# Keys and values of two batch elements as products of float32r halves, made in other places of the first stage

## The chip, the cores and the metric

The kernel runs on one core of a Trainium2 chip, in one launch. The metric is device time in microseconds, the median of three runs. A profile of one execution gives the times of single instructions; they are counted from the first instruction of that execution.

## The reference, cut to what matters

The input x has 4 batch elements of 512 tokens by 512 channels; ctx_2048 has the same shape. Four layers follow one another on x, each with a residual sum and a tanh gate:

```python
x = x + tanh(g_xattn[0]) * wkv_recurrence(w, u, layernorm(x), ctx_2048)   # a scan over tokens, ctx as its values
x = x + tanh(g_ffn[0])   * bitlinear_ffn(layernorm(x), w1, w2, w3)        # 512 -> 2048 -> 512, weights sign * mean
x = x + tanh(g_xattn[1]) * cross_attention(layernorm(x), ctx_2048, ...)   # 16 heads
x = x + tanh(g_ffn[1])   * ternary_linear(rmsnorm(x), gamma, W)
# within cross_attention; the query and output projections are int8 quantised, this one is not:
kv = cond @ wkv.T + bkv          # (4, 512, 512) @ (512, 1024)
k, v = split(kv, 2, axis=-1)
```

The change is in how kv is made for elements 2 and 3 (the third and fourth; counting is from 0).

## The kernel before, in words

All engines work through the four layers and four elements in one long pipeline. The first stage ("boot") holds the start, the recurrence (`wkv_layer`) of elements 0 and 1, the first feed-forward layer (`ffn_layer`) of element 0, the preparation of all weights, and the keys and values of all elements. It ends some 340 us in. Then feed-forward, attention and ternary layers of the elements run beside one another, and reread what boot left in DRAM: signs of weights (`wD`), transposed ctx (`cD`), keys (`kD`) and values (`vD`).

The order of the work is written by hand. `line(generator, parts)` gives a generator and the places of its steps; `event(place, call)` gives one call. `run` always takes the step with the lowest place, so instructions are issued in order of place. `at_unit(n)` is the place of unit n of the feed-forward layer of element 0. That layer has 16 units; a unit is one tile of 128 tokens and one block of 512 hidden channels: two products "up" (`ff_hp`), a gate, a quantisation, a transpose (`tp_ps`) and, two units later, a product "down" (`ff_acc`). Matrix instructions run strictly in that order (`in_turn` and `next_turn` tie each turn to the one before). On ScalarE, VectorE and GpSimd the tile framework orders what is ready, and these run ahead of place: the signs of the last block of w3, place 11.5, are taken at 225.0 us, before unit 10 begins at 235.5. All DMAs named here are issued from SP's queue, in order.

Keys and values (`keys_values`, lines 491 to 527): the weight wkv is transposed once into `wkvT` (f32, 16 KB per partition). ctx of an element is fetched by rows (`fetch`, tile `cn`), transposed on TensorE (`load`, `ct_ps`), copied by ScalarE to `cT` and, for elements 2 and 3, stored to `cD`. A step of keys is four f32 matmuls (128x128 weights by 512 tokens) and a `split` of the result: ScalarE writes the float32r part, VectorE the remainder, both to tile `k_half`. A step of values is four f32 matmuls and one VectorE sum (`V`). Eight steps make one element. For elements 2 and 3 they are spread over the units:

```python
for b, load, over, start in ((2, 0.7, 2.0, 3.6), (3, 9.0, 9.75, 9.8)):
    event(at_unit(load), lambda b=b: context.fetch(b))
    event(at_unit(over), lambda b=b: context.load(b))
    line(late(lambda b=b: context.keys_values(b, "m")), (at_unit(start + 0.2), at_unit(start + 6.0), 8))
```

Three things share buffers with this. `cn` of elements 2 and 3 takes one of the two buffers "wn", through which every block of weights is loaded too (`Weights.load`, line 284). A load waits until the buffer's last reader but one block is done. PSUM results of transposes, keys and values share two banks ("m"). `cT` is one buffer in the pool of boot; element 1 has its own.

Beside this, boot takes signs of the blocks of w1, w2 and w3 on ScalarE (`signs`), sums their magnitudes, turns them by bf16 transposes (`turned`, `wt_ps`), and from unit 11 on loads wq, wp and wf, quantises them on VectorE (`rounded`, `ternary`: lines 218 to 220 are `quantise`), and turns them into `wqT`, `wpT`, `wfT` (`ints_turned`). `output_scales` fills `swp_b` and `bp_b`. These five constants are first written after unit 12.

Of the kernel before, what the change touches and what calls it, by code (L numbers as in the profile page):

```python
# [10 lines left out]
F32 = mybir.dt.float32  # L11
# [10 lines left out]
P = 128  # L22
# [8 lines left out]
def kernel(  # L31
# [69 lines left out]
    wqT = cp.tile([P, NC, D], BF16, name="wqT")  # L101
    wpT = cp.tile([P, NC, D], BF16, name="wpT")
    wfT = cp.tile([P, NC, D], BF16, name="wfT")
# [7 lines left out]
    bp_b = cp.tile([P, D], F32, name="bp_b")  # L111
    gamma_b = cp.tile([P, D], F32, name="gamma_b")
    sq = cp.tile([P, NC], F32, name="sq")
    swp_b = cp.tile([P, D], F32, name="swp_b")
# [159 lines left out]
    class Weights:  # L274
# [134 lines left out]
        def ints_turned(self, key):  # L409
            dst = {"q": wqT, "p": wpT, "f": wfT}[key]  # L410
            yield from self.transposed(self.ints.pop(key), lambda c: dst[:, c, :], 0)

        def output_scales(self):

            pb = bank("pb_ps")
            for j in range(NC):
                transpose(
                    pb[:, j * P : (j + 1) * P],
                    self.sp[:, j : j + 1].to_broadcast([P, P]),
                    ident,  # L420
                )
            nc.vector.tensor_scalar(swp_b, pb, gates[:, 1:2], None, ALU.mult)
# [4 lines left out]
    class Context:  # L427


        def __init__(self, pool):  # L430
# [4 lines left out]
            self.wkvT = pool.tile([P, NC, 2 * D], F32, name="wkvT")  # L435
# [49 lines left out]
        def weights_turned(self, i):  # L485
            wn = self.raw[i]
            for j in range(NC):
                at = i * D + j * P
                self.transposed(self.wkvT[:, :, at : at + P], wn[:, j, :])

        def keys_values(self, b, tag):
# [3 lines left out]
            for g in range(NC):  # L495
                kp = psum_tile("k_ps", tag)
                for c in range(NC):
                    matmul(
                        kp,
                        lhsT=self.wkvT[:, c, g * P : (g + 1) * P],  # L500
# [11 lines left out]
            for t in range(NT):  # L512
                vp = psum_tile("v_ps", "m" if b else tag)
                for c in range(NC):
# [3 lines left out]
                        rhs=self.wkvT[:, c, D : 2 * D],  # L518
# [301 lines left out]
    def attention_layer(b, xb, pool, tiles=range(NT)):  # L820
# [18 lines left out]
        def prepared(t, r):  # L839
# [13 lines left out]
            nc.gpsimd.tensor_tensor(xb[:, t, :], xb[:, t, :], bp_b, ALU.add)  # L853
# [12 lines left out]
        def project(g):  # L866
            qp = bank("q_ps")[:, 0:n]
            for c in range(NC):
                matmul(
                    qp,  # L870
                    lhsT=wqT[:, c, g * P : (g + 1) * P],
# [124 lines left out]
        def project_out(t):  # L996
# [10 lines left out]
            for c in range(NC):  # L1007
                matmul(
                    pp, lhsT=oqT[:, c, :], rhs=wpT[:, c, :], start=(c == 0), stop=(c == NC - 1)
# [5 lines left out]
            nc.vector.scalar_tensor_tensor(y, pp, s[:, 0:1], swp_b, ALU.mult, ALU.mult)  # L1015
# [88 lines left out]
    def ternary(b, xb, pool, t, r, scale=None):  # L1104
# [38 lines left out]
        for c in range(NC):  # L1143
            matmul(fp, lhsT=xT[:, c, :], rhs=wfT[:, c, :], start=(c == 0), stop=(c == NC - 1))
# [55 lines left out]
    with (  # L1200
# [81 lines left out]
        for b, load, over, start in ((2, 0.7, 2.0, 3.6), (3, 9.0, 9.75, 9.8)):  # L1282
            event(at_unit(load), lambda b=b: context.fetch(b))
            event(at_unit(over), lambda b=b: context.load(b))
            line(
                late(lambda b=b: context.keys_values(b, "m")),
                (at_unit(start + 0.2), at_unit(start + 6.0), 8),
# [107 lines left out]
```

## Time and profile before

| | us |
|---|---|
| three runs | 1115.97, 1114.70, 1111.44 |
| median | 1114.7 |
| the profiled execution, whole | 1115.4 |
| its span, first to last instruction | 1113.6 |
| TensorE busy in the span | 946.8 (85%) |
| VectorE busy | 851.9 (76%) |
| ScalarE busy | 704.8 (63%) |
| GpSimd busy | 315.3 (28%) |
| mean granted TensorE clock | 0.953 of full |

How to read it: the engines run beside one another, so busy times do not add up to the span. The time of a matmul in the trace goes from its start to its last result, and the next one starts before that; the time between two starts is what one costs in a row. A clock under 1.00 is what the chip's throttle granted to TensorE. In lists by time, the bracket behind an instruction says how long its engine sat idle and what ended that.

### The profile page before, as it was taken

How to read it: one execution, taken by the hardware profiler on the slowest of the kernel's cores; microseconds unless marked ns; L12 is line 12 of the kernel's file. 1: busy time of each engine (PE TensorE's matmuls, PEld its weight loads, DVE VectorE, ACT ScalarE, POOL GpSimd, SP SyncE). 2: the span in 40 equal slices, each digit the busy share in tenths (PEclk: the TensorE clock that was granted, in tenths of full speed). 3: DMA queues.
4: the chain of work that ended last, by engine and by line, in shares of the span. 5: the costliest groups of instructions: out<-in, count | busy, mean ns of one | idle time of the engine just before them, and what ended most of it. 6: DMA issues, size and time to landing. Idle time of an engine off the chain costs nothing.

```text
span 1113.6 us, 17974 instructions
## 1 busy us (share of the span) xinstructions
PE 946.8 (85%) x6380; PEld 683.5 (61%) x6380; DVE 851.9 (76%) x1642; ACT 704.8 (63%) x1454; POOL 315.3 (28%) x311
## 2 busy tenths in 40 slices
PE   4879998978878978889998777899998989878885
PEld 3345565555546756667776466677776767656652
DVE  4986447779776799988759988877687766679977
ACT  6756655453224676667777667577775677877864
POOL 3822104432105143542214536412113321100000
PEclk8879999998888999999999999999998999989997
DMA  8189854554435655644746544466564653253411
GB/s 283 50 275 319 305 199 147 179 170 152 151 104 170 226 188 161 195 152 158 246 153 209 178 152 152 145 213 199 170 197 152 225 193 109 71 158 106 114 49 39
DMA packets 85673, 189.68 MB, mean 170 GB/s; under 512 B 12240, under 2 KB 36816, under 8 KB 74576
## 3 DMA queue, kind: packets, MB, share of 16 engines
q1 hardware_dynamic: 85584, 188.53, 51.5%
q8 instruction: 51, 0.84, 0.3%
q14 instruction: 38, 0.31, 0.1%
HBM read 148.65 MB, written 39.85 MB: 169 GB/s over the span
## 4 chain that ended last, share of the span: by engine, by line
PE 44%; DVE 25%; ACT 12%; issue 8%; POOL 6%; DMA 3%; SPq 1%; POOLq 0%; ACTq 0%; DVEq 0%
PE ff_hp L162 13%; PE ff_acc L162 6%; PE pt_ps L165 5%; PE o_ps L162 4%; PE s_ps L162 3%; PE v_ps L162 3%; DVE wk_q L620 3%; ACT at_P L929 3%; DVE at_nm L927 3%; ACT at_PT L949 2%; PE k_ps L162 2%; PE tp_ps L165 2%; DVE wk_p L614 2%; DVE qg_i L660 1%; PE qr_ps L165 1%
## 5 line engine op out<-in xcount | busy, mean ns | idle before, releaser
L162 PE MATMUL ff_hp<-wT,xp 128*128 128x512 f32 x1024 | 273.7, 411 | 3.7 <-ACT at_P L929 2.1
L162 PEld LDWEIGHTS ff_hp<-wT,xp 128*128 128x128 f32 x1024 | 197.4, 196 | 52.4 <-ACT at_P L929 3.8
L929 ACT ACTIVATE at_P<-s_ps,at_nm 128x512 f32<-128x512 f32 x256 | 174.6, 689 | 74.6 <-DVE at_nm L927 70.9
L927 DVE TENSOR_REDUCE at_nm<-s_ps 128x1 f32<-128x512 f32 x256 | 165.6, 676 | 37.8 <-PE s_ps L162 37.2
L665 POOL TENSOR_TENSOR ff_z<-qg_b,qg_s 128x512 f32<-128x512 bf16 x64 | 71.4, 1116 | 333.0 <-ACT qg_b L664 286.6
L165 PE MATMUL pt_ps<-ident,at_P 128*128 128x128 f32 x1024 | 141.1, 278 | 17.5 <-ACT at_os L969 6.6
L949 ACT COPY at_PT<-pt_ps 128x512 f32<-128x512 f32 x224 | 124.5, 595 | 39.7 <-PE pt_ps L165 38.5
L165 PEld LDWEIGHTS pt_ps<-ident,at_P 128*128 128x128 f32 x1024 | 113.2, 140 | 45.6 <-issue 9.3
L162 PE MATMUL ff_acc<-wT,hr 128*128 128x512 f32 x512 | 136.9, 408 | 4.9 <-ACT hr L676 3.0
L162 PE MATMUL s_ps<-at_kR,at_qR 128*128 128x512 f32 x256 | 98.8, 455 | 22.2 <-ACT at_P L929 14.6
L162 PEld LDWEIGHTS ff_acc<-wT,hr 128*128 128x128 f32 x512 | 92.6, 190 | 25.5 <-ACT hr L676 4.1
L725 ACT ACTIVATE ff_z<-ff_hp,coef 128x512 f32<-128x512 f32 x64 | 43.9, 687 | 65.8 <-PE ff_hp L162 63.2
L162 PE MATMUL o_ps<-at_PT,at_V 128*32 128x128 f32 x2048 | 72.2, 279 | 1.3 <-DVE hr L677 0.7
L664 ACT CAST qg_b<-qg_i 128x512 bf16<-128x512 int8 x80 | 49.3, 617 | 35.3 <-DVE qg_i L660 27.4
L162 PEld LDWEIGHTS s_ps<-at_kR,at_qR 128*128 128x128 f32 x256 | 46.2, 196 | 38.7 <-ACT at_P L929 23.6
L730 DVE SCALAR_TENSOR_TENSOR ff_z<-ff_hp,coef,ff_z 128x512 f32<-128x512 f32 x64 | 47.5, 743 | 28.2 <-PE ff_hp L162 28.2
L162 PE MATMUL v_ps<-wkvT,cT 128*128 128x512 f32 x128 | 63.8, 646 | 5.6 <-DVE wT L301 2.3
L162 PEld LDWEIGHTS o_ps<-at_PT,at_V 128*32 128x32 f32 x2048 | 53.8, 111 | 23.9 <-issue 12.2
L726 DVE SCALAR_TENSOR_TENSOR ff_z<-ff_z,ff_hp 128x512 f32<-128x512 f32 x64 | 43.4, 678 | 29.7 <-ACT ff_z L725 29.1
L165 PE MATMUL tp_ps<-ident,ff_z 128*128 128x128 f32 x256 | 41.3, 286 | 26.3 <-ACT at_PT L949 11.3
L162 PE MATMUL k_ps<-cT,wkvT 128*128 128x512 f32 x128 | 60.1, 620 | 3.1 <-ACT cT L444 1.4
L676 ACT CAST hr<-tp_ps 128x512 fp32r<-128x512 f32 x64 | 37.6, 587 | 35.8 <-PE tp_ps L165 35.5
(180 smaller groups left out, 1683.1 us busy)
## 6 DMA issues: line engine op xcount, KB each, us to landing
wT<-wD SPq DMA_DIRECT2D x72, 1024.0 KB, 5.3
wn<-in_L_ffn_w_dram SPq DMA_DIRECT2D x18, 1024.0 KB, 6.3
at_kR<-kD SPq DMA_DIRECT2D x128, 128.0 KB, 3.2
at_qR<-qD SPq DMA_DIRECT2D x256, 64.0 KB, 2.3
wD<-wT SPq DMA_DIRECT2D x12, 1024.0 KB, 4.5
kD<-k_half SPq DMA_DIRECT2D x16, 512.0 KB, 3.0
qD<-at_half SPq DMA_DIRECT2D x32, 256.0 KB, 2.1
cn<-in_ctx_dram SPq DMA_DIRECT2D x8, 512.0 KB, 6.3
```

Of the source, the lines that this page charges most:

```text
L162: return in_turn(nc.tensor.matmul(*args, **kwargs))
L165: return in_turn(nc.tensor.transpose(*args))
L620: nc.vector.reciprocal(half, half)
L664: nc.scalar.copy(qb, qi)
L665: nc.gpsimd.tensor_tensor(grouped(src), grouped(qb), s.unsqueeze(2).to_broadcast([P, NG, GS]), ALU.mult)
L676: nc.scalar.copy(part[:, 0, :], pt)
L725: nc.scalar.activation(z, hp, AF.Tanh, scale=coef[:, 0:1])
L726: nc.vector.scalar_tensor_tensor(z, z, 1.0, hp, ALU.add, ALU.mult)
L730: nc.vector.scalar_tensor_tensor(z, hp, coef[:, 1:2], z, ALU.mult, ALU.mult)
L927: nc.vector.tensor_reduce(nm, sp, AX.X, ALU.max, negate=True)
L929: nc.scalar.activation(lanes[k, i, t], sp, AF.Exp, bias=nm, accum_out=sums[k][:, t, i : i + 1],)
L949: made[k] = nc.scalar.copy(dst, blocks(pt))
```

## The change

For elements 2 and 3 keys and values are no longer made by f32 matmuls. wkv and ctx are each written as a float32r part and a remainder, and three float32r products (high by high, high by low, low by high) are summed in PSUM.

- `split_weights(i)`, i = 0 for the key half and 1 for the value half of wkv: 4 ScalarE copies to a tile `w_hi` and 4 VectorE subtractions to `w_lo` (128x512 each); then a DMA of 1 MB copies `w_hi` over the f32 weights. The remainders lie in the memory of `wqT`, `wpT`, `wfT`, `bp_b` and `swp_b`, which are now allocated when first written.
- `fetch_half(b, h)` reads 256 tokens of the transposed ctx back from `cD` (512 KB); `split_half` splits them by two ScalarE copies and a VectorE subtraction over 1024 columns.
- `half_keys_values(b, h)` has four steps: two with the keys of two groups of 128 channels each (24 matmuls over 256 columns, two splits), two with the values of a tile of tokens (12 matmuls over 512 columns, one sum). Key results are stored by DMAs half as large.
- `w_hi`, the pair of ctx halves and the `cT` of elements 2 and 3 all use the one buffer "cT".
- ctx of element 3 is fetched at place 3.0 in place of 9.0, and transposed at 3.5 in place of 9.75. The weights are split at 3.8 and 4.7, and the four half-elements stand at 6.2, 7.9, 9.6 and 11.3, one unit each.

The core of the diff:

```diff
-    wqT = cp.tile([P, NC, D], BF16, name="wqT")
-    wpT = cp.tile([P, NC, D], BF16, name="wpT")
-    wfT = cp.tile([P, NC, D], BF16, name="wfT")
+    turned_ints = {}
...
         def ints_turned(self, key):
-            dst = {"q": wqT, "p": wpT, "f": wfT}[key]
+            name = f"w{key}T"
+            dst = cp.tile([P, NC, D], BF16, name=name, tag=name)
+            turned_ints[key] = dst
             yield from self.transposed(self.ints.pop(key), lambda c: dst[:, c, :], 0)
 
         def output_scales(self):
...
+            swp_b = cp.tile([P, D], F32, name="swp_b", tag="swp_b")
+            bp_b = cp.tile([P, D], F32, name="bp_b", tag="bp_b")
+            turned_ints["scale"], turned_ints["bias"] = swp_b, bp_b
...
-            self.wkvT = pool.tile([P, NC, 2 * D], F32, name="wkvT")
+            self.W = [
+                pool.tile([P, NC, D], F32, name="wkvT", tag=f"wkvT{i}") for i in range(2)
+            ]
+            self.low = {}
...
         def weights_turned(self, i):
             wn = self.raw[i]
             for j in range(NC):
-                at = i * D + j * P
-                self.transposed(self.wkvT[:, :, at : at + P], wn[:, j, :])
+                self.transposed(self.W[i][:, :, j * P : (j + 1) * P], wn[:, j, :])
+
+        def split_weights(self, i):
+
+            W = self.W[i]
+            high = self.pool.tile([P, NC, D], F32R, name="w_hi", tag="cT")
+            for c in range(NC):
+                tag = (("wqT", "wpT"), ("wfT", ("bp_b", "swp_b")))[i][c // 2]
+                if isinstance(tag, tuple):
+                    lo = cp.tile([P, D], F32R, name="w_lo", tag=tag[c % 2])
+                elif c % 2 == 0:
+                    both = cp.tile([P, 2, D], F32R, name="w_lo", tag=tag)
+                    lo = both[:, 0, :]
+                else:
+                    lo = both[:, 1, :]
+                nc.scalar.copy(high[:, c, :], W[:, c, :])
+                nc.vector.tensor_tensor(
+                    lo, W[:, c, :], high[:, c, :].bitcast(F32), ALU.subtract
+                )
+                self.low[i, c] = lo
+                if c % 2:
+                    yield
+            self.W[i] = self.pool.tile([P, NC, D], F32R, name="w_high", tag=f"wkvT{i}")
+            nc.sync.dma_start(out=self.W[i].bitcast(F32), in_=high.bitcast(F32))
+
+        def fetch_half(self, b, h):
+
+            self.pair = self.pool.tile([P, 2, NC, 2 * P], F32, name="c_pair", tag="cT")
+            cut = slice(2 * P * h, 2 * P * (h + 1))
+            nc.sync.dma_start(out=self.pair[:, 0], in_=cD[b][:, :, cut])
+
+        def split_half(self):
+
+            hi, lo = self.pair[:, 0], self.pair[:, 1]
+            nc.scalar.copy(lo.bitcast(F32R), hi)
+            nc.vector.tensor_tensor(lo.bitcast(F32R), hi, lo, ALU.subtract)
+            nc.scalar.copy(hi.bitcast(F32R), hi)
+
+        def half_keys_values(self, b, h):
+
+            hi, lo = self.pair[:, 0], self.pair[:, 1]
+            cut = slice(2 * P * h, 2 * P * (h + 1))
+            store = lambda: None
+
+            def products(out, c, w, ctx):
+                i, w = w.start // D, slice(w.start % D, w.start % D + w.stop - w.start)
+                high = self.W[i][:, c, w], ctx(hi)
+                low = self.low[i, c][:, w], ctx(lo)
+                for n, (x, y) in enumerate(((0, 0), (0, 1), (1, 0))):
+                    weight, context = (high, low)[x][0], (high, low)[y][1]
+                    pair = (context, weight) if i else (weight, context)
+                    matmul(
+                        out,
+                        lhsT=pair[0].bitcast(F32R),
+                        rhs=pair[1].bitcast(F32R),
+                        start=(c == 0 and n == 0),
+                        stop=(c == NC - 1 and n == 2),
+                    )
+
+            for g2 in range(0, NC, 2):
+                kp = psum_tile("k_ps", "m")
+                half = self.pool.tile([P, 2, 2, 2 * P], F32R, name="k_half", tag="k_half", bufs=2)
+                for g in (g2, g2 + 1):
+                    out = kp[:, (g - g2) * 2 * P : (g - g2 + 1) * 2 * P]
+                    for c in range(NC):
+                        products(out, c, slice(g * P, (g + 1) * P), lambda a: a[:, c, :])
+                    split(half[:, g - g2], out, self.bkc[:, g : g + 1])
+                store()
+
+                def store(g2=g2, half=half):
+                    for g in (g2, g2 + 1):
+                        nc.sync.dma_start(
+                            out=kD[b][g][:, :, cut].rearrange("i p t -> p i t"),
+                            in_=half[:, g - g2].bitcast(F32),
+                        )
+
+                yield
+            for j in range(2):
+                t = 2 * h + j
+                vp = psum_tile("v_ps", "m")
+                for c in range(NC):
+                    products(
+                        vp,
+                        c,
+                        slice(D, 2 * D),
+                        lambda a: a[:, c, j * P : (j + 1) * P],
+                    )
+                V = self.pool.tile([P, D], F32, name="V", tag="k_half", bufs=2)
+                nc.vector.tensor_tensor(V, vp, self.bv_b, ALU.add)
+                store()
+                store = lambda t=t, V=V: nc.sync.dma_start(out=vD[b][:, t, :], in_=V)
+                yield
+            store()
 
         def keys_values(self, b, tag):
 
...
-                        lhsT=self.wkvT[:, c, g * P : (g + 1) * P],
+                        lhsT=self.W[0][:, c, g * P : (g + 1) * P],
...
-                        rhs=self.wkvT[:, c, D : 2 * D],
+                        rhs=self.W[1][:, c, :],
...
             event(at_unit(sign), lambda m=m, f=f: made.signs(m, f, m == 2))
             line(made.turned(m, f), (at_unit(end - 0.8), at_unit(end + 0.1), 4))
         event(at_unit(12.0), made.down_scale)
-        for b, load, over, start in ((2, 0.7, 2.0, 3.6), (3, 9.0, 9.75, 9.8)):
+        for b, load, over in ((2, 0.7, 2.0), (3, 3.0, 3.5)):
             event(at_unit(load), lambda b=b: context.fetch(b))
             event(at_unit(over), lambda b=b: context.load(b))
+        for i, start in enumerate((3.8, 4.7)):
             line(
-                late(lambda b=b: context.keys_values(b, "m")),
-                (at_unit(start + 0.2), at_unit(start + 6.0), 8),
+                late(lambda i=i: context.split_weights(i)),
+                (at_unit(start), at_unit(start + 0.4), 3),
+            )
+        for b, h, start, end in (
+            (2, 0, 6.2, 7.2),
+            (2, 1, 7.9, 8.9),
+            (3, 0, 9.6, 10.6),
+            (3, 1, 11.3, 12.3),
+        ):
+            event(at_unit(start - 0.65), lambda b=b, h=h: context.fetch_half(b, h))
+            event(at_unit(start - 0.35), context.split_half)
+            line(
+                late(lambda b=b, h=h: context.half_keys_values(b, h)),
+                (at_unit(start), at_unit(end), 4),
             )
         for key, w, load in (("q", wq, 11.0), ("p", wp, 12.1), ("f", wf, 13.3)):
             event(at_unit(load), lambda key=key, w=w: made.load(key, w))
```

More of the change, by code (lines that the diff above doesn't have):

```diff
@@ L110 @@
     bqc = cp.tile([P, NC], F32, name="bqc")
-    bp_b = cp.tile([P, D], F32, name="bp_b")
     gamma_b = cp.tile([P, D], F32, name="gamma_b")
     sq = cp.tile([P, NC], F32, name="sq")
-    swp_b = cp.tile([P, D], F32, name="swp_b")
     coef = cp.tile([P, 4], F32, name="coef")
@@ L851, in prepared @@
             nc.scalar.copy(sxb[:, t * P : (t + 1) * P], sp)
-            nc.gpsimd.tensor_tensor(xb[:, t, :], xb[:, t, :], bp_b, ALU.add)
+            nc.gpsimd.tensor_tensor(xb[:, t, :], xb[:, t, :], turned_ints["bias"], ALU.add)
             yield True
@@ L870, in project @@
                     qp,
-                    lhsT=wqT[:, c, g * P : (g + 1) * P],
+                    lhsT=turned_ints["q"][:, c, g * P : (g + 1) * P],
                     rhs=xqT[:, c, lo : lo + n],
@@ L1008, in project_out @@
                 matmul(
-                    pp, lhsT=oqT[:, c, :], rhs=wpT[:, c, :], start=(c == 0), stop=(c == NC - 1)
+                    pp, lhsT=oqT[:, c, :], rhs=turned_ints["p"][:, c, :], start=(c == 0), stop=(c == NC - 1)
                 )
@@ L1014, in project_out @@
                 y = row("at_y")
-            nc.vector.scalar_tensor_tensor(y, pp, s[:, 0:1], swp_b, ALU.mult, ALU.mult)
+            nc.vector.scalar_tensor_tensor(y, pp, s[:, 0:1], turned_ints["scale"], ALU.mult, ALU.mult)
             (nc.vector if b > NB - 3 else nc.gpsimd).tensor_tensor(
@@ L1143, in ternary @@
         for c in range(NC):
-            matmul(fp, lhsT=xT[:, c, :], rhs=wfT[:, c, :], start=(c == 0), stop=(c == NC - 1))
+            matmul(fp, lhsT=xT[:, c, :], rhs=turned_ints["f"][:, c, :], start=(c == 0), stop=(c == NC - 1))
         xt = xb[:, t, :]
```

## The prediction

> **What bounds the kernel now.** First the page's 40 slices, to find the changed stage.
>
> ```profile
> PE   4879998978878978889998777899998989878885
> DVE  4986447779776799988759988877687766679977
> ACT  6756655453224676667777667577775677877864
> PEclk8879999998888999999999999999998999989997
> ```
>
> A slice is 27.8 us. All that changes lies in slices 3 to 12, the stage in which the first feed-forward layer runs over 16 units while weights are prepared and keys and values of elements 2 and 3 are made. TensorE is busiest of the engines to slice 9; in slices 8 and 9 (222 to 278 us) VectorE reaches 9 too, and in slices 9 to 12 the granted clock sinks. So I cut the stage at first matmuls of feed-forward units (unit 3 at 137.8 us, 6 at 178.5, 10 at 235.5, 12 at 265.0, 15 at 318.4, the layer after at 344.2) and read busy time in these five stretches, A to E:
>
> ```profile
> 137.80:178.50 40.70, 36.71 (x177) 24.11 (x173) 22.07 (x35) 25.24 (x39) 7.70 (x8) 1.00 0.53 199
> 178.50:235.50 57.00, 49.39 (x227) 32.02 (x225) 39.55 (x53) 29.91 (x47) 20.02 (x21) 1.00 0.44 150
> 235.50:265.00 29.50, 23.39 (x100) 15.62 (x98) 27.55 (x42) 9.67 (x19) 11.02 (x10) 0.94 0.53 187
> 265.00:318.40 53.40, 42.59 (x177) 27.15 (x176) 45.61 (x96) 12.97 (x21) 13.05 (x12) 0.86 0.33 116
> 318.40:344.20 25.80, 20.76 (x78) 13.59 (x76) 15.79 (x42) 6.84 (x12) 8.03 (x9) 0.83 0.55 168
> ```
>
> After length come TensorE, weight loads, VectorE, ScalarE, GpSimd, then clock. A and B are TensorE's (90% and 87%); C is VectorE's (93%); D is shared, VectorE 85%, with TensorE at a clock of 0.86; E is a tail of short chains. A microsecond of TensorE is therefore worth most in A and B, one of VectorE in C and D.
>
> Next, TensorE in order of time, for what a product costs when others follow at once (a duration in the trace overlaps the next one, so I use starts):
>
> ```profile
> 132.16 3.59 PE L162 MATMUL v_ps<-wkvT,cT 128*128 128x512 f32 x8
> 135.59 0.60 PE L165 MATMUL tp_ps<-ident,ff_z 128*128 128x128 f32 x4
> ...
> 193.38 3.98 PE L162 MATMUL ff_hp<-wT,xp 128*128 128x512 f32 x16
> 197.19 0.60 PE L165 MATMUL wy_ps<-ident,wk_e 128*128 128x128 f32 x4
> 197.63 3.60 PE L162 MATMUL v_ps<-wkvT,cT 128*128 128x512 f32 x8
> ...
> 283.21 6.77 PE L162 MATMUL v_ps<-wkvT,cT 128*128 128x512 f32 x8 [0.68 <-ACT wqT L299]
> ...
> 321.91 4.41 PE L162 MATMUL v_ps<-wkvT,cT 128*128 128x512 f32 x8
> 326.16 0.39 PE L165 MATMUL wt_ps<-identb,wi 128*128 128x128 bf16 x4
> 326.36 2.11 PE L162 MATMUL ff_hp<-wT,xp 128*128 128x512 f32 x8
> ```
>
> A step of keys or values (four f32 products, two records each) takes 135.59 - 132.16 = 3.43 us. A float32r product over 512 columns takes (197.19 - 193.38)/16 = 0.238 us. A 128x128 transpose, each with a weight load of its own, takes (197.63 - 197.19)/4 = 0.11 us.
>
> Last, the loads, for what holds the quantisation that fills VectorE in C and D:
>
> ```profile
> 195.54 1.73 SPq L458 DMA_DIRECT2D cn<-in_ctx_dram  x2
> 215.80 0.38 SPq L286 DMA_DIRECT2D wn<-in_L_ffn_w_dram  x1
> 231.11 0.38 SPq L286 DMA_DIRECT2D wn<-in_L_xattn_wq_dram  x1
> ```
> ```profile
> 237.46 2.29 DVE L214 TENSOR_REDUCE w_am<-wn 128x4 f32<-128x2048 f32 x1 [0.63 <-DMA wn<-in_L_xattn_wq_dram]
> ```
>
> wq's load leaves at 231.11, when the fourth element's ctx (cn), loaded at 195.5 into one of two "wn" buffers, has been transposed (230.43 + 0.65). VectorE then waits for wq's data.
>
> **The change, part by part.** *Products.* Out: 16 steps of 3.43 = 54.9 us. In: for keys 192 products over 256 columns, each with its own weight load; no row shows this form. It lies between the transpose's 0.11 us (a load, 128 columns) and the 0.238 us of 512 columns; I take half of the latter, 0.119, since the load of 0.11 fits behind it: 24 per step, 2.86 us. For values 12 per step over 512 columns, 2.86 us. Sum 45.8 us, 9.1 less, if it holds. The upper end is 24 x 0.238 = 5.7 us per key step, 23 us more in all. The Trainium skill (TensorE: Matmul & The Clock Gate, Part 3) says that a weight load overlaps a running matmul only when the row groups differ, which would put load and stream end to end. The trace disagrees: ff_hp loads full 128 rows (187 ns recorded) and still starts a product every 238 ns. By that rule a key step would be near the upper end.
>
> *Places.* Before, one step falls every 0.725 unit from place 3.8 to 15.8: A holds 4 key steps, B 4 value and 1 key, C 2 key, D 1 key and 3 value, E 1 value. After, four bursts of four steps stand from place 6.2 to 12.05: A none, B 10 steps, C 5, D 1, E none.
>
> *Splitting.* ScalarE gets 8 copies of 128x512 (0.59 us, as hr L676) and 8 of 128x1024 (1.05, as wk_e L594): 13 us. VectorE gets 8 subtractions of 0.69 (as V L523) and 4 of 1024 columns at 1.22 (two of 0.69 less a fixed part, by the line from 512 to the 2.29 of 2048): 10.4 us. Halving the key splits doubles their fixed parts: 16 more instructions of some 0.15 us each (the near-empty ones of 128x4 take that) on both engines, 2.4 us or less. So VectorE +13, ScalarE +15 over A to C. In A ScalarE is 62% busy, VectorE 54%: covered by TensorE there. Where that cover goes, as in C, each costs itself.
>
> *ctx sooner.* 16 transposes (4 x 0.44 = 1.8 us of TensorE, 2.4 of ScalarE copies) move from B to A. cn leaves the ring of loads, so wq follows the matrix whose signs end at 215.8, not cn: its load can leave 15 us earlier, and wp and wf after it. wq's quantisation is 2.28 + 4 x (0.48 + 0.41 + 0.41) = 7.5 us of VectorE that can slide from C and D into B, where VectorE has 17 us free. The new DMAs (two of 1 MB within SBUF, four ctx halves back from cD) add some 4 MB to a stage whose DMA share is 0.33 to 0.55; their price is latency, below. Key stores double in number, half in size: 8 more issues of 0.35 us on SP, which is idle between.
>
> *Waits.* All of it uses one buffer, "cT": cD's store of the fourth ctx (7.1 us to landing), split, copy back (1 MB; 4.2 as wD's store to 7.1), split, copy, fetch of a half (3.0 as kD's store to 5.3 as cn's), its split (2 x 1.05 + 1.22). Sum 7.1 + 4 + 5.5 + 4 + 5.5 + 4 + 3.3 = 33 us, from the ctx transposes at place 3.5 to the first keys at 6.2: 2.7 units, at A's 13.6 us each 37 us. It just fits; it fits no longer if A shrinks by more than 4 us. Behind a late split stand, on TensorE, all matmuls in turn; on SP, behind a fetch waiting for the previous half's last product, the weight loads and stores.
>
> *By stretch.*
> A: four steps out, of which the chain of waits carries two (3.70 + 3.45); transposes in. TensorE busy falls to 36.7 - 13.7 + 1.8 = 24.8, ScalarE rises to 25.2 - 2.1 + 2.4 + 4.7 + 2.1 = 32.3. Between -7 and +5; I take -2.5, held up by the chain just named.
> B: TensorE 49.4 - 17.2 - 1.8 + 28.6 = 59.0. With all 7.6 us of present idle kept 66.6, with none 59; VectorE's slack fills some. I take 62.5, +5.5.
> C: TensorE 23.4 - 6.9 + 14.3 = 30.8, VectorE 27.6 + 4 less what slid to B. I take 32, +2.5 (ends +1 and +4).
> D: TensorE 42.6 - 17.8 (the rows' busy time, slow clock included) + 2.9 = 27.7; VectorE 45.6 - 2.8 + 0.7 - up to 7.5 = 36 to 43.5, and the idle waits of VectorE for v_ps (1.9 + 0.6 + 0.2) go. I take 44.4, -9 (ends -14 and -4): what is late next is VectorE.
> E: v_ps at 321.91 stands between the two feed-forward products of the last unit; the second moves up by 326.36 - 321.91 less the transposes, 4.2 us. I take -4 (ends -5 and -2).
> Sum -2.5 + 5.5 + 2.5 - 9 - 4 = -7.5. The profiled execution took 1115.4 (span 1113.6, 1.8 around it), 0.7 above the median of 1114.7, so 1114.7 - 7.5 = 1107. Ends: -24 and +13 together, neither likely.
>
> D's clock speaks against it. The row is v_ps at 283.21: 6.77 us for what takes 3.6, after idle of 3.54 us, at a mean clock of 0.86. The skill's same page (Part 1) says a window of about 3.4 us without work halves the clock. By the row kept as it is, D gives -9; by the rule, with filler gone, each further such window at half clock loses 1.7 us, and two bring D to -5.6 and the sum to -4.
>
> **The rivals.** *Given back, no change (0.27).* TensorE's total falls by 9 us but VectorE's rises by 13, of which 6.7 falls in A, and with five more steps B to D are nearly VectorE's: 39.6 + 27.6 + 45.6 + 10 = 123 of 139.9 us. If nothing slides, D gives -5, B +8, C +3, A -2.5, E -3: 1115. For it: C's 93%; against: the free 17 us in B, which wq reaches earlier.
> *The single buffer, slower (0.28).* TensorE's order is fixed, so the burst at 6.2 waits when the chain of 33 us ends after TensorE reaches it, that is once A is under 36.7 us; then each refill (fetch 3 to 5.3, split 3.3, queueing) must fit 0.95 unit, 13 us. With 4 us in A in place of the gain (+6.5) and 3 at each of three refills (+9): 1107 + 15.5 = 1122.
> *Products over 256 columns dearer (0.03).* At 5.7 us a key step the change doesn't do what it says: 1107 + 23 = 1130.
>
> **How the numbers follow.** Forecast, faster: 0.42. About 0.5%, 5.6 us, is what a measurement of this kernel can tell from no change, so "same" is 1109 to 1120. Faster 0.42, same 0.27, slower 0.28 + 0.03 = 0.31. The range takes D's and A's better ends (1107 - 10) and the buffer rival with 2 us more: 1097 to 1124. The forecast's own range is 1097 to 1109.
>
> **What would show it.** Right: key products start every 0.12 us, value products every 0.24; wq's load leaves near 215 us; no v_ps after unit 13; D and E together are 10 us or more shorter, B is 4 to 8 longer. Wrong: TensorE idle before the first k_ps of a burst, released by ScalarE's or VectorE's c_pair (the buffer); D as long as before with VectorE over 90% (given back); key products at 0.2 us or more.

## The result: slower by 2.3%, and where the time went

The changed kernel took 1139.4 us (median of four runs, 1137.5 to 1142.0) beside 1113.6 us for the kernel before (four runs, 1111.4 to 1116.0): a ratio of 1.023 with an interval of 1.020 to 1.026. The profiled execution took 1142.0, its span is 1140.2. The forecast was 1107, the range ended at 1124. In what follows "over before" is the ratio less one, times 1114 us; here that is +26 us.

The page's slices, which are now 28.5 us long:

```profile
PE   4879974796885988888999788799999989878885
DVE  5976465568688688998677998877677775669977
ACT  6756674434422566676786756677766676887863
PEclk8879995997988899999999999999999999999998
```

In slices 6 to 9 (counted from 0; 171 to 285 us), where TensorE was at 7 to 9 before, it shows 4, 7, 9, 6, and the clock falls to 5 in slice 6. The same five stretches A to E as before, cut at the same feed-forward units (length, then busy time of TensorE, weight loads, VectorE, ScalarE, GpSimd, then clock, DMA share and GB/s):

```profile
138.40:172.70 34.30, 26.68 (x161) 21.04 (x159) 20.48 (x36) 23.82 (x38) 3.58 (x5) 0.93 0.72 258
172.70:277.90 105.20, 73.32 (x364) 61.04 (x362) 67.08 (x90) 45.22 (x71) 32.00 (x31) 0.76 0.40 141
277.90:313.00 35.10, 30.73 (x168) 24.64 (x167) 21.43 (x42) 13.14 (x21) 2.09 (x2) 0.96 0.45 152
313.00:351.40 38.40, 28.49 (x155) 22.15 (x156) 35.48 (x74) 10.33 (x17) 13.57 (x11) 0.88 0.33 115
351.40:373.00 21.60, 15.27 (x71) 10.78 (x68) 16.81 (x46) 6.59 (x12) 9.35 (x10) 0.90 0.56 184
```

Against before A is 6.4 us shorter, B 48.2 longer, C 5.6 longer, D 15.0 and E 4.2 shorter: +28.2 in all. What lies around the stretches gives 1.6 back, which makes the 26.6 us by which the span grew. Nearly all that is lost is lost in B. There TensorE is idle for 31.9 us (7.6 before), and its own 73.3 us of work run at a clock of 0.76.

What TensorE waited for in B, the list's first lines (total us, times, longest):

```profile
PE k_ps L158 <- ACT c_pair L528: 20.6, 3, 12.6
PE k_ps L158 <- DVE k_half L252: 9.9, 7, 2.7
```

These two waits make 30.5 of the 31.9 us. The first is the buffer "cT": TensorE stands before a half until ScalarE's last split of it. The second stands inside the half, six of its seven times between the two groups of a key step. In TensorE's order of time (start, us, and the wait in the bracket):

```profile
189.54 0.80 PE L158 MATMUL k_ps<-c_pair,w_high 128*128 128x256 f32 x2 [12.64 <-ACT c_pair L528]
...
190.35 0.63 PE L158 MATMUL k_ps<-c_pair,w_high 128*128 128x256 f32 x2
190.78 0.41 PE L158 MATMUL k_ps<-c_pair,w_lo 128*128 128x256 f32 x1
190.99 0.63 PE L158 MATMUL k_ps<-c_pair,w_high 128*128 128x256 f32 x2
...
193.56 0.80 PE L158 MATMUL k_ps<-c_pair,w_high 128*128 128x256 f32 x2 [1.08 <-DVE k_half L252]
...
196.28 3.06 PE L158 MATMUL ff_hp<-wT,xp 128*128 128x512 f32 x8
...
199.40 0.48 PE L158 MATMUL k_ps<-c_pair,w_high 128*128 128x256 f32 x2
...
199.83 0.39 PE L158 MATMUL k_ps<-c_pair,w_high 128*128 128x256 f32 x2
200.06 0.28 PE L158 MATMUL k_ps<-c_pair,w_lo 128*128 128x256 f32 x1
200.18 0.40 PE L158 MATMUL k_ps<-c_pair,w_high 128*128 128x256 f32 x2
...
202.13 0.50 PE L158 MATMUL k_ps<-c_pair,w_high 128*128 128x256 f32 x2 [1.08 <-DVE k_half L252]
```

Between the groups of the last pair, ScalarE in order of time:

```profile
201.09 0.47 ACT L251 ACTIVATE k_half<-k_ps,bkc 128x256 fp32r<-128x256 f32 x1 [4.09 <-PE k_ps L158]
```

and VectorE half a microsecond later:

```profile
201.59 0.48 DVE L252 SCALAR_TENSOR_TENSOR k_half<-k_ps,bkc,k_half 128x256 fp32r<-128x256 f32 x1
```

The two groups of a key step share one bank tile of PSUM ("kp"). The second group's first product writes that tile, so it waits until the first group's split has read it: ScalarE at 201.09, then VectorE at 201.59, then TensorE at 202.13. At full clock three products take 200.18 - 199.83 = 0.35 us, 0.117 each; after the long wait 190.99 - 190.35 = 0.64, 0.213 each. Of the 16 key groups seven run at the slow pace from end to end, and one in part.

How a split comes late: ScalarE's order of time in front of the first half,

```profile
181.95 1.03 ACT L526 CAST c_pair<-c_pair 128x1024 fp32r<-128x1024 f32 x1
188.45 1.04 ACT L528 CAST c_pair<-c_pair 128x1024 fp32r<-128x1024 f32 x1 [5.46 <-DVE c_pair L527]
```

and VectorE's:

```profile
180.51 3.33 DVE L715 RECIPROCAL wk_q<-wk_q 128x256 f32<-128x256 f32 x2
185.47 1.23 DVE L674 TENSOR_TENSOR_SCAN wk_o<-wc,wk_k 128x512 f32<-128x512 f32 x1 [1.63 <-POOL wk_p L683]
186.61 0.67 DVE L720 TENSOR_TENSOR wk_e<-wk_e,wk_q 128x512 f32<-128x512 f32 x1
187.19 1.22 DVE L527 TENSOR_TENSOR c_pair<-c_pair 128x1024 fp32r<-128x1024 f32 x1
```

ScalarE had its first cast done at 183.0. VectorE came to the subtraction at 187.2, behind the recurrence of element 1, in which it even sat idle for 1.63 us. Last, SP's queue in order of time:

```profile
171.12 0.48 SPq L515 DMA_DIRECT2D w_high<-w_hi  x1
176.42 0.60 SPq L521 DMA_DIRECT2D c_pair<-cD  x1
...
214.80 0.55 SPq L521 DMA_DIRECT2D c_pair<-cD  x1
...
246.12 0.38 SPq L282 DMA_DIRECT2D wn<-in_L_xattn_wq_dram  x1
```

The first fetch leaves 5.3 us after the copy back of the high weights, which had to free the buffer. The second leaves at 214.80, 1.2 us after the first half's last product has ended, right behind the store of its values. wq's load leaves at 246.1, not near 215: the signs of the block before it end at 246.1 (ScalarE, 244.18 + 1.91).

### The profile page after: what moved, and what is told of

Read it like the earlier page. It is cut to its first block, busy times and chain, and to the rows that moved or that the text cites. A ratio compares the mean times of both kernels' runs of the same rounds, so it can differ in the third digit from the quotient of the medians.

```text
span 1140.2 us, 18387 instructions
## 1 busy us (share of the span) xinstructions
PE 948.3 (83%) x6540; PEld 710.8 (62%) x6540; DVE 862.1 (76%) x1662; ACT 718.6 (63%) x1478; POOL 315.9 (28%) x311
## 4 chain that ended last, share of the span: by engine, by line
PE 47%; DVE 22%; ACT 13%; issue 7%; POOL 6%; DMA 5%; SPq 1%; POOLq 0%; ACTq 0%; DVEq 0%
PE ff_hp L158 13%; PE ff_acc L158 5%; PE pt_ps L161 5%; PE k_ps L158 4%; PE o_ps L158 4%; PE s_ps L158 4%; PE v_ps L158 3%; ACT at_P L1024 3%; ACT at_PT L1044 2%; DVE wk_q L715 2%; DVE at_nm L1022 2%; PE tp_ps L161 2%; PE qr_ps L161 2%; DVE wk_p L709 2%; DVE qg_i L755 1%
## 5 line engine op out<-in xcount | busy, mean ns | idle before, releaser
L158 PEld LDWEIGHTS ff_hp<-wT,xp 128*128 128x128 f32 x1024 | 199.7, 199 | 49.2 <-ACT at_P L1024 3.8
L1022 DVE TENSOR_REDUCE at_nm<-s_ps 128x1 f32<-128x512 f32 x256 | 165.6, 676 | 37.5 <-PE s_ps L158 36.8
L825 DVE SCALAR_TENSOR_TENSOR ff_z<-ff_hp,coef,ff_z 128x512 f32<-128x512 f32 x64 | 47.5, 742 | 29.5 <-PE ff_hp L158 29.4
L771 ACT CAST hr<-tp_ps 128x512 fp32r<-128x512 f32 x64 | 37.5, 586 | 41.0 <-PE tp_ps L161 40.7
L161 PE MATMUL tp_ps<-ident,ff_z 128*128 128x128 f32 x256 | 41.3, 286 | 24.2 <-ACT at_PT L1044 11.0
L158 PE MATMUL k_ps<-c_pair,w_high 128*128 128x256 f32 x128 | 33.3, 360 | 33.4 <-ACT c_pair L528 21.3
L715 DVE RECIPROCAL wk_q<-wk_q 128x256 f32<-128x256 f32 x32 | 54.4, 1719 | 2.6 <-POOL wk_p L703 1.4
```

The costliest lines, as they stand in the source:

```text
L158: return in_turn(nc.tensor.matmul(*args, **kwargs))
L161: return in_turn(nc.tensor.transpose(*args))
L715: nc.vector.reciprocal(half, half)
L771: nc.scalar.copy(part[:, 0, :], pt)
L825: nc.vector.scalar_tensor_tensor(z, hp, coef[:, 1:2], z, ALU.mult, ALU.mult)
L1022: nc.vector.tensor_reduce(nm, sp, AX.X, ALU.max, negate=True)
```

## The experiments

Length of each stretch in us, cut at the same units, and the time over before with the ends of its interval (the ratio of each kernel is to runs of before on the same chip):

| kernel | A | B | C | D | E | median | over before |
|---|---|---|---|---|---|---|---|
| before | 40.7 | 57.0 | 29.5 | 53.4 | 25.8 | 1113.6 | |
| after | 34.3 | 105.2 | 35.1 | 38.4 | 21.6 | 1139.4 | +26 (22 to 29) |
| e1, splits last | 35.0 | 87.8 | 41.3 | 37.5 | 21.3 | 1129.0 | +14 (7 to 20) |
| e2, two buffers | 36.7 | 85.7 | 34.3 | 38.6 | 21.8 | 1125.1 | +10 (7 to 13) |
| e3, both | 35.7 | 73.8 | 38.4 | 38.3 | 21.6 | 1116.9 | +1 (-2 to 5) |
| e4, ctx sooner alone | 47.0 | 51.5 | 29.4 | 54.2 | 24.9 | 1116.6 | +2 (0 to 5) |
| e5, f32 in bursts | 29.4 | 74.8 | 41.7 | 38.2 | 21.3 | 1114.4 | 0 (-2 to 2) |
| e6, halves spread | 47.8 | 66.9 | 35.4 | 38.6 | 21.6 | 1117.3 | +3 (1 to 5) |
| e7, one product | 35.0 | 59.3 | 26.6 | 47.2 | 22.2 | 1099.6 | -15 (-18 to -12) |
| e8, no remainders | 32.9 | 78.8 | 35.2 | 37.5 | 22.5 | 1114.2 | 0 (-2 to 3) |
| e9, GpSimd subtracts | 36.8 | 81.5 | 37.6 | 37.5 | 21.3 | 1123.0 | +9 (6 to 12) |
| e10, f32 in e3's form | 33.0 | 81.3 | 42.4 | 40.3 | 21.3 | 1125.2 | +11 (9 to 14) |
| e11, high parts only | 33.1 | 64.0 | 28.5 | 46.0 | 22.3 | 1102.7 | -12 (-14 to -9) |
| e12, whole elements | 31.8 | 58.0 | 29.7 | 47.5 | 22.1 | 1097.6 | -18 (-21 to -15) |

**The three theories of the loss.** R: the refill of the one buffer. B: the bubble between the two groups of a key step. V: VectorE is full anyway, and time taken from either wait comes back elsewhere. Later expectations name their theories by letters too: P for the places of the products, S for the splitting, L and C for what cheaper products are worth; each says what it means where it first stands.

e1, both groups multiplied before either is split:

```diff
+                outs = [kp[:, i * 2 * P : (i + 1) * 2 * P] for i in range(2)]
                 for g in (g2, g2 + 1):
-                    out = kp[:, (g - g2) * 2 * P : (g - g2 + 1) * 2 * P]
                     for c in range(NC):
-                        products(out, c, slice(g * P, (g + 1) * P), lambda a: a[:, c, :])
-                    split(half[:, g - g2], out, self.bkc[:, g : g + 1])
+                        products(outs[g - g2], c, slice(g * P, (g + 1) * P), lambda a: a[:, c, :])
+                for g in (g2, g2 + 1):
+                    split(half[:, g - g2], outs[g - g2], self.bkc[:, g : g + 1])
```

> The changed kernel, with the two key groups of a step multiplied one after the other and both split behind them; all else as in the changed kernel (1139.4 us). Theory R (refill: the changed kernel loses its time where TensorE waits for the one buffer of ctx halves, 21.3 us of waits for c_pair, and in the slow clock behind each of them): the 12.1 us of waits inside key steps go, the rest stays, so 1127 to 1137. Theory B (bubble: the wait of the second group for the split of the first, 1.1 to 2.7 us in each of 8 key steps, is what breaks the bursts and keeps the clock down): 1139 less 12 us of waits less most of the 14 us of slow clock, 1113 to 1122. Theory V (the added work of VectorE and ScalarE, 13 and 15 us, is the loss): 1139 within 3.

Measured 1129.0. From e1's list of TensorE's waits over A to E, the line for the splits of ctx:

```profile
PE k_ps L158 <- ACT c_pair L528: 16.7, 4, 12.7
```

The refills still wait for 16.7 us (21.3 in after), 12.7 of it at the first. Waits for splits of keys fall from 12.1 to 7.7 us: none stands inside a step any more, and two are left behind a step. So most of the 10 us gained (12 by the two ratios) are the bubble's, with the slow clock behind it. The time lies in R's range; V falls, and B alone (1113 to 1122) falls too.

e2, the first half of each element in memory of its own (that of x of element 2, which is loaded later), so that it is fetched and split ahead:

```diff
-            self.pair = self.pool.tile([P, 2, NC, 2 * P], F32, name="c_pair", tag="cT")
+            pool, tag = (self.pool, "cT") if h else (st, "x2")
+            pair = pool.tile([P, 2, NC, 2 * P], F32, name="c_pair", tag=tag, bufs=1)
...
-            event(at_unit(start - 0.65), lambda b=b, h=h: context.fetch_half(b, h))
-            event(at_unit(start - 0.35), context.split_half)
+            event(at_unit(start - 2.0), lambda b=b, h=h: context.fetch_half(b, h))
+            event(at_unit(start - 0.9), lambda b=b, h=h: context.split_half(b, h))
```

> The changed kernel, with the halves h = 0 of ctx in a second buffer (the memory that later takes x of the third element), each half fetched 2.0 units and split 0.9 units ahead of its products; the products, their places and the work of VectorE and ScalarE are the same. Theory R: the waits for c_pair (21.3 us) go, and the clock behind them (up to 14 us) returns: 1104 to 1120. Theory B: 1134 or more, since the bubbles stay. Theory V: 1139 within 3.

Measured 1125.1, 14 us less than after. The head of e2's list of the same waits:

```profile
PE k_ps L158 <- DVE k_half L252: 19.2, 10, 4.1
```

No wait for c_pair is left, and the bubble has grown from 12.1 (over A to E) to 19.2 us: in the longest, 4.07 us, VectorE runs a scan and a reciprocal of the recurrence (1.97 and 1.72 us) before it comes to the split. R's range (1104 to 1120) was too hopeful, B's (1134 or more) is out.

e3 has both edits.

> Both edits together: a second buffer for ctx halves, fetched earlier, and splits behind both key groups. Theories R and B add: 1098 to 1112, below the kernel before (1113.6). Theory V: 1136 or more.

Measured 1116.9: 22.5 us less than after, where the two gains alone add up to 24.7. So the two waits are two causes, about 14 and 10 us (16 and 12 by the ratios, 24.5 together), each with the slow clock that follows it. Waits for splits of keys are not gone: 8.5 us of them stand in e3 before the second key step of a half or before its values. But 1116.9 is no gain over before, and above the expected 1098 to 1112. Next question: why is nothing left of the 9 us that the products save?

**Is it the places?** e4 is before with ctx of element 3 fetched and transposed at 3.0 and 3.5, stored, and read back at 9.75; the f32 steps stay where they were.

```diff
-        for b, load, over, start in ((2, 0.7, 2.0, 3.6), (3, 9.0, 9.75, 9.8)):
+        for b, load, over, start in ((2, 0.7, 2.0, 3.6), (3, 3.0, 3.5, 9.8)):
...
+            if b == 3:
+                event(at_unit(9.75), lambda b=b: context.again(b))
```

> The kernel before (1113.6 us), with f32 products in their old places, but ctx of the fourth element fetched at place 3.0 and transposed at 3.5 into memory of x of the third element, stored, and read back (1 MB) into cT at 9.75: the part 'ctx loaded sooner' alone. If the 15 us that stretch D (units 12 to 14) lost in the changed kernel come from wq's earlier load, D loses 5 us or more here too: 1104 to 1110. If they come from the products moved out of D, D stays as it was: 1111 to 1117.

Measured 1116.6. wq's load left at 220.5 in place of 231.1, and D and E together are 79.1 us, as before (79.2). An earlier wq is worth nothing here; D's gain is from the products that moved out.

e5 adds two bursts of f32 steps to that, 6.2 to 8.9 and 9.6 to 12.3, with no splitting at all; ctx of element 3 is read back at 9.0.

```diff
-                (at_unit(start + 0.2), at_unit(start + 6.0), 8),
+                (at_unit(start), at_unit(start + 2.7), 8),
```

> The kernel before with f32 products, ctx of the fourth element sooner (as in e4), and the 16 steps in two bursts of 8 at places 6.2 to 8.9 and 9.6 to 12.3, in place of 3.8 to 15.8: the change of places alone, with no splits of weights or ctx and no refill of halves. Theory P (places: what e3 still loses in units 6 to 11 is crowding of the products, whatever their form): 16 steps of 3.43 us in the bursts against 2.86 in e3 (1116.9 us) make 1122 to 1130. Rival S (splitting: the 13 and 15 us of added work on VectorE and ScalarE eat what the products save): 1112 to 1119, no slower than e3.

Measured 1114.4, in the range of S, with no sign of P. The five stretches of e5, with the same columns as above:

```profile
138.70:168.00 29.30, 24.86 (x159) 19.49 (x157) 16.08 (x28) 19.14 (x29) 3.48 (x4) 1.00 0.81 293
168.00:242.90 74.90, 65.84 (x253) 38.74 (x250) 53.18 (x74) 37.90 (x60) 24.18 (x25) 0.98 0.44 161
242.90:284.50 41.60, 36.35 (x132) 20.53 (x130) 28.23 (x47) 11.44 (x18) 9.55 (x10) 1.00 0.45 158
284.50:322.70 38.20, 25.58 (x145) 19.92 (x144) 34.24 (x72) 9.52 (x16) 13.44 (x10) 0.85 0.28 97
322.70:344.00 21.30, 15.21 (x71) 11.02 (x69) 16.80 (x46) 6.59 (x11) 9.83 (x10) 0.90 0.65 197
```

A, D and E lose 31 us and B and C gain 30. The burst costs in B and C what it frees in A, D and E, to a microsecond. Places are worth nothing either way, and e6 says the same of e3, with its halves at 5.2 to 7.0, 7.0 to 8.8, 8.9 to 10.6 and 10.7 to 12.4:

```diff
-            (2, 0, 6.2, 7.2),
-            (2, 1, 7.9, 8.9),
-            (3, 0, 9.6, 10.6),
-            (3, 1, 11.3, 12.3),
+            (2, 0, 5.2, 7.0),
+            (2, 1, 7.0, 8.8),
+            (3, 0, 8.9, 10.6),
+            (3, 1, 10.7, 12.4),
```

> e3 (two buffers, splits behind both groups) with the four halves spread without gaps over places 5.2 to 12.4, one step every 0.45 unit in place of bursts of four at every 0.25. Theory P: TensorE's idle in stretch A is filled and units 6 to 9 shorten; 4 to 10 us less than e3, 1107 to 1113, below the kernel before (1114.2). Rival S: as e3, 1114 to 1119.

Measured 1117.3, again where S had it.

**Is it the products?** e7 keeps one product of the three, high by high, and all of e3's splitting.

```diff
-                for n, (x, y) in enumerate(((0, 0), (0, 1), (1, 0))):
+                for n, (x, y) in enumerate(((0, 0),)):
```

> e3 with only the high by high product of the three; the two products with a remainder are left out, all splits stay. TensorE has 30 us less to do in units 6 to 12. Theory P: these units are TensorE's, so 18 to 30 us less than e3: 1087 to 1099. Rival S: they are VectorE's (93 us busy of 112 in units 6 to 11 of e3), so less than 12 us: 1105 to 1116.

Measured 1099.6, 17 us less than e3 for 30 us less of products. That lies between the two ranges: TensorE's time counts, by about half of what is taken out.

e10 goes the other way: e3's form, but one f32 product of the high parts in place of the three, about 9 us more.

```diff
-                for n, (x, y) in enumerate(((0, 0), (0, 1), (1, 0))):
+                for n, (x, y) in enumerate(((0, 0),)):
...
-                        lhsT=pair[0].bitcast(F32R),
-                        rhs=pair[1].bitcast(F32R),
+                        lhsT=pair[0].bitcast(F32),
+                        rhs=pair[1].bitcast(F32),
```

> The kernel e3_both with its splitting, buffers, places and steps unchanged, but each sum of three float32r products replaced by one f32 product of the high parts (the remainders are made and not used). By before's rows an f32 step takes 3.43 us where three float32r products take 2.86, so TensorE's products cost some 9 us more. Theory L (a microsecond of products is worth what e7_one_product showed, 17 us for 30): 1119 to 1124, some 5 us over e3_both's 1116.9. Theory C (cheaper products are paid back, since TensorE then waits more and runs at a lower clock): 1113 to 1118, with a mean granted clock in the stage nearer to the 0.95 of e5_f32_bursts than to the 0.91 of e3_both.

Measured 1125.2, 8.4 us over e3 by the medians (10 by the two ratios). That is just above the range of L. Theory C falls: the cheaper products are not paid back in clock, they bring about all of their 9 us (6 to 14 by the intervals, where e7's 30 us brought half). But then e10 has the same f32 products as e5, in nearly the same places, and is 11 us slower. So what eats the saving is the form: splits of weights and ctx, copies back, fetches and halves. TensorE in order of time, key steps of e10:

```profile
175.11 3.72 PE L158 MATMUL k_ps<-c_pair,w_high 128*128 128x256 f32 x16 [0.50 <-DVE hr L779]
183.53 5.41 PE L158 MATMUL k_ps<-c_pair,w_high 128*128 128x256 f32 x16 [2.63 <-DVE k_half L252]
...
208.57 3.72 PE L158 MATMUL k_ps<-c_pair,w_high 128*128 128x256 f32 x16 [0.95 <-DVE wT L297]
218.38 5.30 PE L158 MATMUL k_ps<-c_pair,w_high 128*128 128x256 f32 x16 [4.00 <-DVE k_half L252]
```

and of e5:

```profile
171.88 3.70 PE L162 MATMUL k_ps<-cT,wkvT 128*128 128x512 f32 x8
179.52 3.70 PE L162 MATMUL k_ps<-cT,wkvT 128*128 128x512 f32 x8
187.49 3.70 PE L162 MATMUL k_ps<-cT,wkvT 128*128 128x512 f32 x8 [0.78 <-DVE wT L301]
192.88 3.60 PE L162 MATMUL k_ps<-cT,wkvT 128*128 128x512 f32 x8
```

A warm step costs the same in both (3.7 us). In halves, the second key step of element 2's two halves waits 2.6 and 4.0 us for the splits of keys, and its products then take 5.3 to 5.4 us at a lower clock.

**Which part of the form?** e8 leaves out the remainders: no subtraction, one ctx cast less, all three products from high parts.

```diff
-                nc.vector.tensor_tensor(
-                    lo, W[:, c, :], high[:, c, :].bitcast(F32), ALU.subtract
-                )
...
-            nc.scalar.copy(lo.bitcast(F32R), hi)
-            nc.vector.tensor_tensor(lo.bitcast(F32R), hi, lo, ALU.subtract)
```

> The kernel e3_both with the remainders left out: no subtraction for the weights or the ctx halves, and one ScalarE copy less per ctx half; the three products per sum are all made of the high parts, so TensorE's work is unchanged. It leaves out 8 subtractions of 512 columns and 4 of 1024 on VectorE (some 10 us) and 4 copies of 1024 on ScalarE (4 us). Theory S (the splitting work eats what the products save): 1104 to 1110, that is 7 to 13 us under e3_both's 1116.9. Theory P (the crowded places of the products hold the stage): 1114 to 1118.

Measured 1114.2, 2.7 us less than e3 by the medians and 1 by the ratios. Theory S, which e5 and e6 had seemed to bear out, falls: 10 us of VectorE taken out are worth 1 to 3 us, by the intervals hardly more than 5. e9 moves the same subtractions to GpSimd:

```diff
-                nc.vector.tensor_tensor(
+                nc.gpsimd.tensor_tensor(
...
-            nc.vector.tensor_tensor(lo.bitcast(F32R), hi, lo, ALU.subtract)
+            nc.gpsimd.tensor_tensor(lo.bitcast(F32R), hi, lo, ALU.subtract)
```

> The kernel e3_both with the subtractions of the weights' and the ctx halves' splits on GpSimd in place of VectorE; the same numbers come out. Theory S: 1107 to 1113, since some 10 us of VectorE's work go to an engine that is less than a third busy in the stage. Rival (GpSimd takes longer for the same subtraction, so that the halves come later or its own work of the recurrence is late): 1115 to 1122.

Measured 1123.0, 6 us more than e3 by the medians, 8 by the ratios, and above both ranges. GpSimd in order of time, in e9, and VectorE beside its second row:

```profile
171.83 5.42 POOL L508 TENSOR_TENSOR w_lo<-wkvT,w_hi 128x512 fp32r<-128x512 f32 x4 [1.32 <-ACT w_hi L507]
189.75 2.37 POOL L529 TENSOR_TENSOR c_pair<-c_pair 128x1024 fp32r<-128x1024 f32 x1
```
```profile
190.35 1.80 DVE L758 TENSOR_SCALAR qg_s<-qg_s 128x8 f32<-128x8 f32 x1
```

Four subtractions of 512 columns take 5.42 us (2.47 on VectorE), one of 1024 takes 2.37 (1.23). VectorE is not simply relieved: the instruction shown, 0.16 us long in the median of its 80 runs, ends here at 192.15, just behind GpSimd's at 192.12. TensorE never waits for a half of ctx in e9; its waits for splits of keys before a second key step grow from 3.12 and 1.77 us in e3 to 4.41 and 3.99. By what way the slower subtraction lengthens them, no run takes apart.

e11 is e7 without the remainders that it doesn't use, and e12 is e11 with whole elements: one fetch, keys in four steps of 512 columns with one split each, as before the change.

> The kernel e7_one_product without what it makes and doesn't use: no remainders, so one float32r product, one ScalarE copy for each half of ctx and each part of wkv, no subtraction. The products of the remainders are left out, so keys and values of elements 2 and 3 are those of float32r roundings of ctx and wkv. If remainders cost what e8_no_remainders showed (3 us under e3_both): 1095 to 1099. If, with fewer products, VectorE and ScalarE hold the stage more: 1088 to 1094. If nothing: 1099 to 1102.

```diff
-        for b, h, start, end in (
-            (2, 0, 6.2, 7.2),
...
+        for b, start in ((2, 6.2), (3, 9.6)):
+            event(at_unit(start - 2.0), lambda b=b: context.fetch_whole(b))
+            event(at_unit(start - 0.9), lambda b=b: context.round_whole(b))
+            line(
+                late(lambda b=b: context.whole_keys_values(b)),
+                (at_unit(start), at_unit(start + 2.7), 8),
+            )
```

> The kernel e11_high_only with whole elements in place of halves of 256 tokens: one fetch and two roundings of 1024 columns per element, keys in four steps of four float32r products over 512 columns with one split each, values as before, at places 6.2 to 8.9 and 9.6 to 12.3. TensorE's products take the same time (16 products of 256 or 8 of 512 columns); half as many key splits, stores and fetches remain. The products of the remainders are left out as in e11_high_only. e10_f32_same_shape was 10.9 us over e5_f32_bursts with the same f32 products: if that lies in the halves (two groups to a bank, twice the splits, a fetch for each half): 1091 to 1097. If it lies in the splitting of the weights and ctx and in the single ring of buffers, which this kernel keeps: 1100 to 1105.

e11 took 1102.7, no gain over e7 and just above all three ranges: again the remainders' work is worth nothing that can be measured. e12 took 1097.6, just above the first of its two ranges and 6 us less than e11 by the ratios (2 to 10 by the intervals). So about half of the form's 11 us lies in the halves, if a kernel with one product and no remainders may stand for it. The other half stays open: the casts and copies back of the weights, the read-back of ctx, or the burst's start behind them; no run takes these out one by one. e12 beats both kernels, with a ratio of 0.984 (0.981 to 0.987), but its keys and values are of rounded ctx and wkv.

## Why the prediction was wrong

The forecast's sum was -7.5. By stretch, taken and measured: A -2.5 and -6.4; B +5.5 and +48.2; C +2.5 and +5.6; D -9 and -15.0; E -4 and -4.2. **The step that failed is B**, and it failed in three places; a fourth miss, the price of the form, stands in the account below.

*The chain of waits on "cT".* The text set it at 33 us and said that it fits no longer once A is under 36.7 us; A became 34.3. The condition was right, and the forecast should have seen that its own reason for a shorter A (four steps out) works against its cover. The cover was overrated besides: 37 us were counted from the ctx transposes, which began at 143.8, but the chain starts with the store of their result at 149.1, and TensorE was through with the work ahead of the first key step at 176.9, 27.8 us later. The chain also grew: 40.4 us from the cD store at 149.1 to the first key product at 189.5. Of the excess 4.3 us are the split: 7.6 us from the start of its first cast to the first product, where 3.3 stood in the sum, since VectorE came to it late. 40.4 less 27.8 is the 12.6 us that TensorE came too early. The buffer rival named the place and the sign, with the direction of the wait, but took 3 us for each refill and 4 in A; the four waits are 12.6, 3.7, 4.3 and 0.7 us.

*The bubble, which no step named.* "24 per step, 2.86 us" treats a step of two key groups as one run of products. The diff showed both groups in one bank tile and a split after each: the second group's write follows the first one's read, over two engines. Eight such waits cost 10.3 us over A to E (a ninth of the same kind, 1.75 us, stands between two key steps), and e1 gives 10 us back.

*Work priced at full clock.* B's busy time was put at 59.0 us and came to 73.3. The extra 14 us are not more instructions but a clock of 0.76. The Trainium skill (TensorE: Matmul & The Clock Gate, Part 1) speaks of a window of about 3.4 us for the fall and the same, busy, for the return. The traces agree on the length: the clock changes in steps of 3.41 us (last section), and each wait of 3.26 us or more ahead of a key or value product was followed by half clock. The prediction applied the rule to D, where work was taken away, and not to B, where its own rival put waits.

*What was right.* The products: at full clock one starts every 0.117 us, for the 0.119 taken, and e10 beside e3 shows that the saving of 9.1 us is real and reaches the end of the kernel (8.4 to 10 us). The rival of dearer products is out. D and E shrink because f32 steps leave them, by more than was taken (-19 for -13). For the places the forecast had no term of its own; e5 shows that they give nothing: -31 and +30. wq's load sliding forward was in D's reason and is worth nothing (e4); in after it did not slide at all, since the block before it came late. Two slips of the text bear on nothing: its low ends add up to -23, not -24, and of slices 8 and 9 VectorE reaches 9 in slice 9 alone.

VectorE's row for wq in after, in order of time, has a wait of 0.15 us for the load where before had 0.63:

```profile
252.91 2.29 DVE L210 TENSOR_REDUCE w_am<-wn 128x4 f32<-128x2048 f32 x1 [0.15 <-DMA wn<-in_L_xattn_wq_dram]
```

The account that the runs support: products -9 or -10 (e10 to e3), places 0 (before to e5), the form of splits and halves +11 (e5 to e10), bubble +10 and refills +14 (after to e1 and e2). That sums to 25 or 26, and 26 was measured. The first three terms are steps of one chain of kernels, from before over e5 and e10 to e3, and must meet e3's time; what the sum tests is that bubble and refills add up. The prediction had the first term, none for the second, priced the third as busy time of engines with room, and the last two at zero in the likeliest case.

The rival "given back" had the right size for a kernel without the two waits: e3 is where it put the time, 1115, though not by a full VectorE, as e8 shows.

## What to carry to other kernels

When a change frees time ahead of a burst, set the burst's own chain of preparation against the shortened stretch, with queueing on each engine that it crosses, and not against the old one. Groups of products that share a tile and are evicted one by one should all be multiplied ahead of the first eviction (a tile for each was not tried here); a wait of 1 us between them also keeps a slow clock slow. Cheaper arithmetic pays only if its operands come without a new form: here three products saved 9 us and their splits, halves and copies cost 11. One product over whole elements beat the kernel before, with rounded values.

## What the runs showed of the hardware

A float32r product over 256 columns, with a 128x128 weight load of its own, starts every 0.117 us at full clock, half of the 0.23 to 0.24 us of 512 columns: the load costs nothing beside it at this width either. An f32 step over 256 columns costs what it costs over 512 in the same work (3.7 us for 16 and for 8 records).

Every group of key or value products that followed a wait of 3.26 us or more began at half clock (0.21 us a product over 256 columns, 0.43 over 512, in after, e1, e2 and e3); after shorter waits both were seen, full clock after 3.12 us and half after 2.10 us in e3. In e1, 24 products in a row were still slow 5.1 us after the wait and the feed-forward product behind them was not; in after, with one pause of 1.08 us among the same products, the feed-forward product that began 6.7 us after the wait still took 0.36 us each (196.28 to 199.19 for eight; 0.24 is the full pace). The trace of the granted clock tells why. It is cut here where the clock changes (after, then e1; columns as for A to E):

```profile
191.74:195.15 3.41, 2.33 (x11) 2.03 (x11) 0.48 (x1) 0.47 (x1) 0.00 (x0) 0.50 0.22 76
195.15:198.56 3.41, 3.41 (x13) 2.93 (x12) 0.49 (x1) 0.47 (x1) 0.00 (x0) 0.50 0.05 17
198.56:201.97 3.41, 2.49 (x20) 1.97 (x18) 2.49 (x5) 0.47 (x1) 0.00 (x0) 1.00 0.19 66
```
```profile
193.30:196.72 3.42, 3.42 (x18) 3.42 (x18) 0.00 (x0) 0.00 (x0) 0.00 (x0) 0.50 0.02 5
196.72:200.13 3.41, 3.38 (x23) 2.68 (x23) 2.21 (x5) 0.95 (x2) 0.00 (x0) 1.00 0.31 111
```

In every run here the clock changes in this stage only in steps of 3.41 us. From 165 to 300 us in all fourteen kernels, a step at half clock was followed by full clock only if TensorE had idled in it for 0.51 us or less, and a step at full clock by half clock only if TensorE had idled in it for 1.77 us or more (the longest idle that did no harm was 1.89). So the pause of 1.08 us left the clock alone in the warm pair at 202.13, but in the step from 191.74 it kept the clock at half for one step more: there a bubble costs more than its own length. It also explains e3: its 2.10 us lie in one step, its 3.12 us are split by the end of a step into 1.84 and 1.28.
